# Graph convolution on one core: where the selection matrices are built, and for how many tiles edge_attr is loaded

## The chip, the cores and the metric

The kernel runs on one core of a Trainium2 chip. The metric is the device time of one execution in microseconds (us), the median of the runs shown. One further execution was taken with the hardware profiler; where the text speaks of a row, a wait or a timeline, it means that execution.

Five engines of the core take part. TensorE (PE in the profile, PEld for its weight loads) multiplies matrices into PSUM. VectorE (DVE) and ScalarE (ACT) do elementwise work. GpSimd (POOL) issues the gathers. SyncE (SP) issues most of the other transfers.

## The reference

One layer of a graph network. There are N = 12500 nodes with 160 features each (64 scalars and 32 vectors of 3), and 400000 edges, sorted by their target node.

```python
h_s, h_v = s @ lin1_ws / 8, v @ lin1_wv / sqrt(32)        # per node, times the node's attribute
w  = silu(edge_scalars @ fc_w1 / 8) @ fc_w2 / 8           # per edge: 64 -> 64 -> 224 weights
es, ev = h_s[edge_src], h_v[edge_src]
e0, e1 = edge_attr[:, :1], edge_attr[:, 1:4]
m_s1 = w1 * es * e0
m_s2 = w4 * (ev . e1) / 3
m_v1 = (w2 * es) (x) e1
m_v2 = w3 * ev * e0
m_v3 = w5 * cross(ev, e1) / 2
agg  = segment_sum(messages, edge_dst) / 4
pre  = self_connection(x) + lin2(agg)                     # per node
out  = layernorm(x + gated(pre))
```

(Scales and shapes are shortened. Layernorm has no learned weights.)

## The kernel before

**Tiles.** 128 edges are a tile, one edge in each partition. Five tiles (TB) are a block of 640 edges; there are 625 blocks. Since edges are sorted by target, the targets of a block fall into a window of W = 32 nodes, whose first node is computed on the chip. Four tiles are a quad (Q), and the main loop (L607) has one step for each quad, 782 in all. The quads are taken from chunks of 20 tiles: two sides of SIDE = 10 tiles each. A quad has two tiles of one side and two of the other, so that the two halves of the 128 partitions of `es` hold two runs of edges; a quad therefore usually touches two blocks. A chunk has 5 steps.

**Before the loop.** A table `h_tab` of all nodes' h is computed and written to DRAM. `rel`, for each edge the distance of its target from its block's first node, is computed once. The loop starts at about 113 us.

**A step n of the loop.** `hide(n + 1)` computes the hidden layer for a later step: the load of `es` (L278, on SP), two matmuls `ph` (L290), silu (L292). `gather` (L299) issues four indirect DMAs on GpSimd, one for each tile, into `hg`, a pool of four buffers. `weights` (L311) makes the 224 weights of each edge in PSUM: the tile `pw` has 128 x 4 x 256 numbers, of which columns 0 to 223 of each tile are used; there are two such buffers, of two banks each. `products` on VectorE multiplies `pw` and `hg` (L319, and three times L328) into `pr`. The multiplication by edge_attr and the sum over edges are one matmul: `sel` holds, for each edge and each of the four edge_attr components, a row of 32 numbers that is zero but for the column of its target, where it has the component. `add_tile` (L357) multiplies `sel` of a tile (as weights) with `pr` into the sums `pa` of a pair of blocks. This is done for the quad of the step before (`sum_up(*before)`), so that TensorE does pw(n) ahead of pa(n-1).

**Selection.** `select` works on one block: `oh` (L338) compares `rel` with 0 to 31 for five tiles, 128 x 160 numbers, into SBUF; `sel` (L341) multiplies that by edge_attr, 128 x 640 numbers. Four buffers of `sel` are kept. A list `order` says at which step a block is first needed. In each step, after the products and after the add below, blocks needed at once are selected; else one block is, if it is needed up to two steps ahead. So most steps have a selection and some have none.

**Closing a pair of blocks.** When a pair's sums are complete they are copied to SBUF (`sa`, L361), transposed (`pt` L369, copied as `tt` L370) in a later step, and every eight blocks the second linear map is applied (`po`, L378, copied as `os` L382). Then `add` (L387) adds one block a step to its window of `acc`, which holds the sums of all nodes in SBUF; the window's start is loaded into registers between L319 and L328.

**Finishing nodes.** When all blocks that reach a set of 512 nodes are added, `finish` handles it in pieces, one a step, by `go_on`: `turn` transposes 128 nodes of `acc` on TensorE (`pp`, L406) and scales them (`z`, L407), and then gates, residual, moments and normalization on VectorE and ScalarE follow, with a load of x (L394) and a store of the result (L437) on SP. There are 98 such turns. Every 30 steps a piece of the self connection is added to `acc` (L505 to L511).

**Loads of edge_attr.** For each group of 125 tiles `group` loads the indices of the gathers (L466) and, next to them, edge_attr (L468): 25 loads of 250 KB, with 2000 bytes in each partition.

**Order.** On TensorE, VectorE, ScalarE and GpSimd the instructions run in the order in which the program is written (`manual_schedule`, L603). SP runs its transfers in program order too, ahead of the others as far as the buffers allow. A redo path after the loop handles blocks whose targets don't fit into a window; it isn't entered with this data.

Of the kernel before, what the change touches and what calls it, by code (L numbers as in the profile page):

```python
# [10 lines left out]
F32 = mybir.dt.float32  # L11
I32 = mybir.dt.int32
# [3 lines left out]
OP = mybir.AluOpType  # L16
# [4 lines left out]
P = 128  # L21
# [4 lines left out]
TB = 5  # L26
BG = 25
EB = TB * P
EG = BG * EB
W = 32  # L30
Q = 4
SIDE = 2 * TB
# [4 lines left out]
NWT = 224  # L37
# [27 lines left out]
def gnn_kernel(  # L65
# [21 lines left out]
    nc = tc.nc  # L87
# [5 lines left out]
    GT = BG * TB  # L93
# [15 lines left out]
    for i in range(2):  # L109
        r = slice(S + i * V, S + (i + 1) * V)  # L110
# [204 lines left out]
    def products(pool, pw, hg, n, between=()):  # L315

        pr = pool.tile([P, Q, NPR], F32, name="pr")

        nc.vector.tensor_mul(  # L319
            pr[:, :n, 6 * V:10 * V].rearrange("p t (k c) -> p t k c", k=2),  # L320
            pw[:, :n, :2 * S].rearrange("p t (k c) -> p t k c", k=2),
            hg[:, :n, None, :S].to_broadcast([P, n, 2, S]))
        for f in between:
            f()

        for k, (first, step) in enumerate(((1, 2), (4, -2), (10, 1))):
            full = pr[:, :n, first * V:]
            nc.vector.tensor_mul(  # L328
                bass.AP(tensor=full.tensor, offset=full.offset,
                        ap=[full.ap[0], full.ap[1], [step * V, 3], [1, V]]),  # L330
                pw[:, :n, None, 2 * S + k * V:2 * S + (k + 1) * V].to_broadcast([P, n, 3, V]),
                hg[:, :n, S:].rearrange("p t (i c) -> p t i c", i=3))
        return pr

    def select(pool, r, e):

        oh = pool.tile([P, TB, W], F32, name="oh")
        nc.vector.tensor_tensor(oh, r[:, :, None].to_broadcast([P, TB, W]),  # L338
                                iota[:, None, :].to_broadcast([P, TB, W]), op=OP.is_equal)
        sel = pool.tile([P, TB, 4, W], F32, name="sel", bufs=4)  # L340
        nc.vector.tensor_mul(sel, oh[:, :, None, :].to_broadcast([P, TB, 4, W]),  # L341
                             e[:, :, :, None].to_broadcast([P, TB, 4, W]))
        return sel

    def cleared(psum):
# [5 lines left out]
    def add_tile(pa, sel, t, pr, start, stop):  # L351

        for k, (first, step, count) in enumerate(SUMS):
            span = pr[:, first * V:]
            a = bass.AP(tensor=span.tensor, offset=span.offset,
                        ap=[span.ap[0], [step[0] * V, count[0]], [step[1] * V, count[1]], [1, V]])
            nc.tensor.matmul(pa[k * W:(k + 1) * W], sel[:, t, k], a, start=start, stop=stop)  # L357
# [96 lines left out]
    with tc.tile_pool(  # L454
# [5 lines left out]
    ) as pa_ps, tc.tile_pool(name="misc_ps", bufs=2, space=PSUM) as misc_ps:  # L460
        groups = {}

        def group(g):
            if g not in groups:
                idx = loads.tile([P, GT], I32, name="idx")
                nc.sync.dma_start(idx, src[g])  # L466
                eat = loads.tile([P, GT, 4], F32, name="eat")
                nc.sync.dma_start(eat.rearrange("p t k -> p (t k)"),  # L468
                                  ea[g].rearrange("p t k -> p (t k)"))
                groups[g] = idx, eat  # L470
            return groups[g]

        def index(t):
            return group(t // GT)[0][:, t % GT:t % GT + 1]


        chunks = [((c, SIDE), (c + SIDE, SIDE)) for c in range(0, NB * TB - 2 * SIDE + 1, 2 * SIDE)]
# [8 lines left out]
        ess, hids = {}, {}  # L486
# [12 lines left out]

        CHN = 500  # L500

        def self_connection(c0):
# [10 lines left out]
        sels, order = {}, []  # L513
        for n, (_, _, tiles) in enumerate(steps):
            for t, _, _ in tiles:
                b = t // TB
                if b not in [x for _, x in order[-4:]]:
                    order.append((n, b))

        def choose(b):  # L520
            g, k = divmod(b, BG)
            sels[b] = select(edge, rel[:, b * TB:(b + 1) * TB],
                             group(g)[1][:, k * TB:(k + 1) * TB])

        left_of = {b: TB for b in range(NB)}
        pas = {}
# [33 lines left out]
        def sum_up(tiles, pr):  # L560
            for slot, (t, _, _) in enumerate(tiles):
                b = t // TB
                pa, place, blocks = sums_of(b)
                n = TB - left_of[b]
                last = n == TB - 1 and all(x == b or not left_of[x] for x in blocks)
                add_tile(pa[:, place], sels[b], t % TB, pr[:, slot], start=False, stop=last)
                left_of[b] -= 1
                if left_of[b] == 0:
                    sels.pop(b)
# [32 lines left out]

        with tc.manual_schedule(engines={ENG.PE, ENG.DVE, ENG.Activation, ENG.Pool}):  # L603
            hide(0)
            before = None
            pieces = list(range(0, N, CHN))
            for n, (c, i, tiles) in enumerate(steps):  # L607
                hide(n + 1)
                hg = gather(deep, [index(t) for t, _, _ in tiles])
                now, later = later, []  # L610
                pw = weights(pw_ps, hids[c, i // 2], [(half, u - i // 2 * 4) for _, half, u in tiles])
                ready = []
                pr = products(edge, pw, hg, len(tiles), [lambda: ready.extend(add_up(1))])
                for a in ready:
                    add(*a)

                need = [b for m, b in order if m <= n]
                todo = [b for _, b in order if b not in sels]
                for b in need:
                    choose(b)  # L620
                order = [(m, b) for m, b in order if b not in need]
                if not need and order and order[0][0] <= n + 2:
                    choose(order.pop(0)[1])
                go_on()
                for f in now:
                    f()
                if before is not None:
                    sum_up(*before)
                before = (tiles, pr)
                if n % 30 == 6 and pieces:  # L630
                    self_connection(pieces.pop(0))
            assert not pieces
            sum_up(*before)
            while later:
                later.pop(0)()
            while adds:
                for a in add_up(1):
                    add(*a)
            while doing or to_do:
                go_on()  # L640
# [88 lines left out]
```

## Time and profile before

| What | Value |
|---|---|
| Median of 3 runs (lowest to highest) | 5651.8 us (5649.6 to 5672.22) |
| Profiled execution, its own time | 5669.53 us |
| Its span | 5667.7 us |
| Mean granted clock of TensorE | 0.816 |
| TensorE busy (weight loads) | 74% (39%) |
| GpSimd busy | 54% |
| VectorE busy | 47% |
| ScalarE busy | 14% |
| Mean DMA traffic | 73 GB/s |

A row of the groups reads: line, engine, operation, what it writes and reads, partitions x elements, count; then the busy time in us and the mean length of one in ns; then how long the engine was idle just before these instructions, and what ended most of it. In a row of waits the numbers are the total in us, the number of waits and the longest. A line of the timeline has the start and the length in us, and in brackets the idle time ahead of it and what ended it. Idle time that "remote" ended is put down to no instruction of the records.

### The profile page before, as it was taken

Reading aid. Unit: us, or ns where it says so; the run is one execution under the profiler, and the core shown is the slowest. Engines: PE = TensorE matmul, PEld = TensorE weight load, DVE = VectorE, ACT = ScalarE, POOL = GpSimd, SP = SyncE. Lnnn points to the kernel's source line nnn. Section 1 sums busy time; section 2 is a strip of 40 time slices with the busy share of each in tenths; the row PEclk is TensorE's granted clock in tenths of the full one; section 3 lists DMA queues with packets and bytes.
Section 4 is the critical chain, followed back from the end, with each engine's and each line's share of the span. In section 5 each row is a group of like instructions: output and inputs, shape, how many; then the busy total and the mean of one; then the engine's idle time right before and its main releaser. Section 6 shows DMA issues by size and latency. Waiting matters only on the chain.

```text
span 5667.7 us, 89792 instructions
## 1 busy us (share of the span) xinstructions
PE 4182.8 (74%) x36179; PEld 2227.6 (39%) x36179; DVE 2642.3 (47%) x5628; ACT 809.3 (14%) x1639; POOL 3051.9 (54%) x3134
## 2 busy tenths in 40 slices
PE   6777777767777767777777777777776767777776
PEld 5334433333344434334333333433333433434343
DVE  4444444444444444444444444444444444444444
ACT  0111111111111111111111111111111111111111
POOL 3555555555555555555555555555555555555553
PEclk7788887888888878888888788887887888888787
DMA  6222222222222222222222222222222322232221
GB/s 172 68 72 73 72 72 66 73 74 65 76 76 67 74 68 74 74 70 74 72 74 73 63 76 69 73 77 68 75 72 63 82 67 73 71 79 69 68 69 46
DMA packets 232392, 416.39 MB, mean 73 GB/s; under 512 B 64580, under 2 KB 160592, under 8 KB 231713
## 3 DMA queue, kind: packets, MB, share of 16 engines
q0 software_dynamic: 150000, 256.20, 17.3%
q1 hardware_dynamic: 65972, 142.43, 9.9%
q10 hardware_dynamic: 15994, 11.93, 0.8%
q8 instruction: 285, 4.67, 0.3%
q14 instruction: 141, 1.16, 0.1%
HBM read 394.32 MB, written 16.00 MB: 72 GB/s over the span
## 4 chain that ended last, share of the span: by engine, by line
PE 31%; another core or an unknown queue 8%; issue 6%; DVE 3%; ACT 3%; DVEq 0%; DMA 0%; POOL 0%; ACTq 0%; POOLq 0%
PE pa L357 13%; PE pw L311 6%; PE ph L290 4%; PE po L378 3%; PE pt L369 2%; DVE pr L328 2%; ACT tt L370 1%; PE pa L348 1%; ACT hid L292 1%; DVE pr L319 0%; PE pp L406 0%; PE psc L510 0%; ACT L292 0%; DVEq L582 0%
## 5 line engine op out<-in xcount | busy, mean ns | idle before, releaser
L299 POOL DMA_INDIRECT hg<-h_tab,idx x3125 | 3029.5, 969 | 2562.8 <-DVE pr L328 962.0
L357 PE MATMUL pa<-pr,sel 128*32 128x192 f32 x25000 | 1813.8, 395 | 312.7 <-issue 298.8
L319 DVE TENSOR_TENSOR pr<-pw,hg 128x512 f32<-128x512 f32 x782 | 539.1, 689 | 2648.7 <-remote 1400.2
L357 PEld LDWEIGHTS pa<-pr,sel 128*32 128x32 f32 x25000 | 888.3, 127 | 1060.3 <-issue 768.8
L328 DVE TENSOR_TENSOR pr<-pw,hg 128x384 f32<-128x384 f32 x2346 | 1158.2, 549 | 5.7 <-issue 4.9
L311 PE MATMUL pw<-w,hid 64*128 64x224 f32 x6250 | 990.0, 429 | 48.3 <-issue 38.8
L369 PE MATMUL pt<-ident,sa 128*96 128x128 f32 x1250 | 317.8, 344 | 814.6 <-ACT tt L370 418.6
L311 PEld LDWEIGHTS pw<-w,hid 64*128 64x128 f32 x6250 | 645.2, 219 | 585.8 <-issue 530.2
L341 DVE TENSOR_TENSOR sel<-oh,eat 128x640 f32<-128x640 f32 x625 | 517.8, 828 | 168.2 <-PE pw L311 51.2
L290 PE MATMUL ph<-es,w 128*128 128x512 f32 x940 | 552.0, 673 | 10.8 <-issue 8.3
L369 PEld LDWEIGHTS pt<-ident,sa 128*96 128x96 f32 x1250 | 124.7, 144 | 1000.5 <-ACT tt L370 496.0
L361 ACT COPY sa<-pa 128x384 f32<-128x384 f32 x313 | 149.5, 478 | 2085.0 <-PE pa L357 1042.7
L292 ACT ACTIVATE hid<-ph 128x512 f32<-128x512 f32 (+1 forms) x470 | 247.0, 526 | 1242.9 <-PE ph L290 855.1
L378 PE MATMUL po<-tt,l 96*96 96x256 f32 (+1 forms) x1738 | 401.7, 383 | 9.6 <-issue 8.7
L378 PEld LDWEIGHTS po<-tt,l 96*96 96x96 f32 x1738 | 274.5, 164 | 127.1 <-issue 47.6
L370 ACT COPY tt<-pt 96x256 f32<-96x256 f32 x626 | 229.3, 366 | 588.0 <-PE pt L369 361.1
L290 PEld LDWEIGHTS ph<-es,w 128*128 128x128 f32 x940 | 165.8, 219 | 198.1 <-issue 184.7
L406 PE MATMUL pp<-ident,acc 96*128 96x96 f32 x196 | 44.9, 325 | 239.6 <-DVE acc L387 218.9
L338 DVE TENSOR_TENSOR oh<-rel,iota 128x160 f32<-128x160 int16 x625 | 196.3, 314 | 0.0
L382 ACT COPY os<-po 96x512 f32<-96x512 f32 (+1 forms) x79 | 45.6, 577 | 714.9 <-PE po L378 485.1
L387 DVE TENSOR_TENSOR acc<-acc,os 96x64 f32 x625 | 132.7, 212 | 12.6 <-ACT os L382 7.9
L406 PEld LDWEIGHTS pp<-ident,acc 96*128 96x128 f32 x196 | 23.8, 170 | 273.3 <-issue 187.5
(61 smaller groups left out, 794.7 us busy)
## 6 DMA issues: line engine op xcount, KB each, us to landing
es<-in_es_t_dram SPq DMA_DIRECT2D x312, 320.0 KB
hg<-h_tab,idx POOLq DMA_INDIRECT x3125
h_tab<-ht ACTq DMA_DIRECT2D x8, 960.0 KB
xt<-in_x_dram SPq DMA_DIRECT2D x24, 320.0 KB
out_dram<-y SPq DMA_DIRECT2D x24, 320.0 KB
eat<-in_ea_dram SPq DMA_DIRECT2D x25, 250.0 KB
xv<-in_xv_t_dram SPq DMA_DIRECT2D x25, 187.5 KB
xs<-in_xs_t_dram SPq DMA_DIRECT2D x25, 125.0 KB
```

What stands on the lines that cost most here:

```text
L290: nc.tensor.matmul(ph[:k, c], w1[:k, :k], es[:k, t0 * P + c0 * P:t0 * P + c1 * P], start=True, stop=True)
L292: nc.scalar.activation(hid[:k, c], ph[:k, c], AF.Silu, scale=1.0 / math.sqrt(64))
L299: nc.gpsimd.indirect_dma_start(out=hg[:, t, :], out_offset=None, in_=h_tab, in_offset=bass.IndirectOffsetOnAxis(ap=i, axis=0))
L311: nc.tensor.matmul(pw[:, t, :NWT], hid[r, c * P:(c + 1) * P], w2[r], start=True, stop=True)
L319: nc.vector.tensor_mul(pr[:, :n, 6 * V:10 * V].rearrange("p t (k c) -> p t k c", k=2), pw[:, :n, :2 * S].rearrange("p t (k c) -> p t k c", ...
L328: nc.vector.tensor_mul(bass.AP(tensor=full.tensor, offset=full.offset, ap=[full.ap[0], full.ap[1], [step * V, 3], [1, V]]), pw[:, :n, None ...
L338: nc.vector.tensor_tensor(oh, r[:, :, None].to_broadcast([P, TB, W]), iota[:, None, :].to_broadcast([P, TB, W]), op=OP.is_equal)
L341: nc.vector.tensor_mul(sel, oh[:, :, None, :].to_broadcast([P, TB, 4, W]), e[:, :, :, None].to_broadcast([P, TB, 4, W]))
L357: nc.tensor.matmul(pa[k * W:(k + 1) * W], sel[:, t, k], a, start=start, stop=stop)
L369: nc.tensor.transpose(pt[:, half, b], sa[:, b, half * V3:(half + 1) * V3], ident)
L370: nc.scalar.copy(tt[:, half, :, at_b:at_b + nb].rearrange("c k b n -> c b k n"), pt[:, half, :nb].rearrange("c b (k n) -> c b k n", k=4))
L378: nc.tensor.matmul(po[:, k, :nb], l2[:, terms[to, part, half]], tt[:, half, part, :nb], start=(n == 0), stop=(n == len(of) - 1))
```

## The change

The kernel after has a new function `select_quad`, which does the selection of just the quad of the step. The one-hot numbers of its four tiles (128 x 128) are written into columns 224 to 255 of the same `pw` tile in PSUM that holds the quad's weights. From there `sel` is made in two instructions, one for each side (two tiles, 128 x 256 numbers each), with edge_attr as the other input; `sel` has two buffers now. It stands straight after the products and ahead of the add. The list of blocks to be selected and the selection ahead are gone; a step's `sel` goes with its `pr` to `sum_up`. `select` remains for the redo path, with one buffer each.

Edge_attr is loaded for a chunk of 20 tiles at a time by `load_parts`, into three buffers, right behind the chunk's two loads of `es` on SP: 326 loads, of which 300 have ten tiles of one side (128 rows of 160 bytes). Indices are still loaded for 125 tiles.

```diff
     def select(pool, r, e):
-        oh = pool.tile([P, TB, W], F32, name="oh")
+        oh = pool.tile([P, TB, W], F32, name="oh", bufs=1)
...
-        sel = pool.tile([P, TB, 4, W], F32, name="sel", bufs=4)
+        sel = pool.tile([P, TB, 4, W], F32, name="sel1", bufs=1)
...
+    def select_quad(pool, pw, tiles, eat):
+        n = len(tiles)
+        step = tiles[-1][0] - tiles[0][0] - 1 if n == Q else 1
+        r = rel[:, tiles[0][0]:]
+        sides = 2 if n == Q else 1
+        each = n // sides
...
+        nc.vector.tensor_tensor(
+            pw[:, :n, NWT:].rearrange("p (h u) w -> p h u w", h=sides),
+            bass.AP(tensor=r.tensor, offset=r.offset, ap=[r.ap[0], [step, sides], [1, each], [0, W]]),
+            iota[:, None, None, :].to_broadcast([P, sides, each, W]), op=OP.is_equal)
+        sel = pool.tile([P, Q, 4, W], F32, name="sel")
+        for h in range(sides):
+            k = slice(h * each, (h + 1) * each)
+            u = tiles[h * each][2]
+            nc.vector.tensor_mul(
+                sel[:, k], pw[:, k, None, NWT:].to_broadcast([P, each, 4, W]),
+                eat[:, h, u:u + each, :, None].to_broadcast([P, each, 4, W]))
+        return sel
...
-        def group(g):
-            if g not in groups:
-                idx = loads.tile([P, GT], I32, name="idx")
-                nc.sync.dma_start(idx, src[g])
-                eat = loads.tile([P, GT, 4], F32, name="eat")
-                nc.sync.dma_start(eat.rearrange("p t k -> p (t k)"),
-                                  ea[g].rearrange("p t k -> p (t k)"))
...
+        def load_parts(sides):
+            eat = loads.tile([P, 2, SIDE, 4], F32, name="eat", bufs=3)
+            for half, (t, n) in enumerate(sides):
+                at_t = 0
+                while at_t < n:
+                    g, k = divmod(t + at_t, GT)
+                    m = min(n - at_t, GT - k)
+                    nc.sync.dma_start(eat[:, half, at_t:at_t + m], ea[g, :, k:k + m])
+                    at_t += m
+            return eat
...
                 ess[c] = load_hidden(loads, edges)
+                eats[c] = load_parts(chunks[c])
...
-                add_tile(pa[:, place], sels[b], t % TB, pr[:, slot], start=False, stop=last)
+                add_tile(pa[:, place], sel, slot, pr[:, slot], start=False, stop=last)
...
                 pr = products(edge, pw, hg, len(tiles), [lambda: ready.extend(add_up(1))])
+                sel = select_quad(edge, pw, tiles, eats[c])
                 for a in ready:
                     add(*a)
-
-                need = [b for m, b in order if m <= n]
-                todo = [b for _, b in order if b not in sels]
-                for b in need:
-                    choose(b)
-                order = [(m, b) for m, b in order if b not in need]
-                if not need and order and order[0][0] <= n + 2:
-                    choose(order.pop(0)[1])
                 go_on()
...
-                    sum_up(*before)
-                before = (tiles, pr)
+                    sum_up(*before)
+                before = (tiles, pr, sel)
```

More of the change, by code (lines that the diff above doesn't have):

```diff
@@ L335, in select @@
     def select(pool, r, e):
-        oh = pool.tile([P, TB, W], F32, name="oh")
+        oh = pool.tile([P, TB, W], F32, name="oh", bufs=1)
         nc.vector.tensor_tensor(oh, r[:, :, None].to_broadcast([P, TB, W]),
                                 iota[:, None, :].to_broadcast([P, TB, W]), op=OP.is_equal)
-        sel = pool.tile([P, TB, 4, W], F32, name="sel", bufs=4)
+        sel = pool.tile([P, TB, 4, W], F32, name="sel1", bufs=1)
         nc.vector.tensor_mul(sel, oh[:, :, None, :].to_broadcast([P, TB, 4, W]),
                              e[:, :, :, None].to_broadcast([P, TB, 4, W]))
+        return sel
[5 more added lines that the diff above has]
+        each = n // sides
+        assert [t - tiles[0][0] for t, _, _ in tiles] == [h * step + u for h in range(sides) for u in range(each)]
+        nc.vector.tensor_tensor(
[9 more added lines that the diff above has]
+                eat[:, h, u:u + each, :, None].to_broadcast([P, each, 4, W]))
         return sel
@@ L461, in gnn_kernel, with index @@
         groups = {}
-        def group(g):
+        def index(t):
+            g = t // GT
             if g not in groups:
-                idx = loads.tile([P, GT], I32, name="idx")
-                nc.sync.dma_start(idx, src[g])
-                eat = loads.tile([P, GT, 4], F32, name="eat")
-                nc.sync.dma_start(eat.rearrange("p t k -> p (t k)"),
-                                  ea[g].rearrange("p t k -> p (t k)"))
[L470 to L474, printed above, removed]
+                groups[g] = loads.tile([P, GT], I32, name="idx")
+                nc.sync.dma_start(groups[g], src[g])
+            return groups[g][:, t % GT:t % GT + 1]
+        def load_parts(sides):
[8 more added lines that the diff above has]
+            return eat
         chunks = [((c, SIDE), (c + SIDE, SIDE)) for c in range(0, NB * TB - 2 * SIDE + 1, 2 * SIDE)]
@@ L484, in gnn_kernel @@
                 steps.append((c, i, [(sides[half][0] + u, half, u) for half, u in slots]))
-        ess, hids = {}, {}
+        ess, eats, hids = {}, {}, {}
         def hide(n):
@@ L511, in self_connection @@
                 nc.vector.tensor_add(acc[:, k, c0:c0 + cn], acc[:, k, c0:c0 + cn], p[:, :cn])
[L513 to L523, printed above, removed]
         left_of = {b: TB for b in range(NB)}
@@ L558, in output, with sum_up @@
             adds.extend((b, os, k) for k, b in enumerate(blocks))
-        def sum_up(tiles, pr):
+        def sum_up(tiles, pr, sel):
             for slot, (t, _, _) in enumerate(tiles):
@@ L565, in sum_up @@
                 last = n == TB - 1 and all(x == b or not left_of[x] for x in blocks)
-                add_tile(pa[:, place], sels[b], t % TB, pr[:, slot], start=False, stop=last)
+                add_tile(pa[:, place], sel, slot, pr[:, slot], start=False, stop=last)
                 left_of[b] -= 1
                 if left_of[b] == 0:
-                    sels.pop(b)
                     for k, (p, blocks) in enumerate(pair):
```

## The prediction

> **What bounds the kernel now.** First the page's busy times, to see whether any engine is full.
>
> ```profile
> PE 4182.8 (74%) x36179; PEld 2227.6 (39%) x36179; DVE 2642.3 (47%) x5628; ACT 809.3 (14%) x1639; POOL 3051.9 (54%) x3134
> PE 31%; another core or an unknown queue 8%; issue 6%; DVE 3%; ACT 3%; DVEq 0%; DMA 0%; POOL 0%; ACTq 0%; POOLq 0%
> ```
>
> None is. The second line is the chain that ended last: TensorE leads it, VectorE has 3%. So work added on VectorE counts only where TensorE or GpSimd waits for it. Next, the page's costliest groups: the gathers, and the five VectorE groups that a step runs.
>
> ```profile
> L299 POOL DMA_INDIRECT hg<-h_tab,idx x3125 | 3029.5, 969 | 2562.8 <-DVE pr L328 962.0
> L319 DVE TENSOR_TENSOR pr<-pw,hg 128x512 f32<-128x512 f32 x782 | 539.1, 689 | 2648.7 <-remote 1400.2
> L341 DVE TENSOR_TENSOR sel<-oh,eat 128x640 f32<-128x640 f32 x625 | 517.8, 828 | 168.2 <-PE pw L311 51.2
> L406 PE MATMUL pp<-ident,acc 96*128 96x96 f32 x196 | 44.9, 325 | 239.6 <-DVE acc L387 218.9
> L338 DVE TENSOR_TENSOR oh<-rel,iota 128x160 f32<-128x160 int16 x625 | 196.3, 314 | 0.0
> L387 DVE TENSOR_TENSOR acc<-acc,os 96x64 f32 x625 | 132.7, 212 | 12.6 <-ACT os L382 7.9
> ```
>
> The loop runs 782 steps from about 113 us on, so a step takes about 7.05 us. VectorE stands idle 2648.7 us before the first product of a step (3.4 us each): the cover for what the change adds to it. GpSimd needs 4 gathers, each 0.95 us and a gap of 0.30, 5.0 us a step: it is not the bound either. "Remote" before L319 is not this step's gather, which landed 13 us or more earlier; it is TensorE's signal for pw, recorded as issued and not yet answered. Third, the waits:
>
> ```profile
> DVE pr L319 <- remote: 1400.2, 267, 19.1
> PE pp L406 <- DVE acc L387: 218.9, 66, 8.5
> ```
>
> Columns are total us, times, longest. The second line is the only large wait of TensorE on an operation that the change moves: 66 waits of 3.3 us. Last, the timeline of one step with such a wait (start, length, engine and line):
>
> ```profile
> 3001.59 0.69 DVE L319 TENSOR_TENSOR pr<-pw,hg 128x512 f32<-128x512 f32 x1 [6.50 <-PE pw L311]
> 3002.28 1.49 DVE L328 TENSOR_TENSOR pr<-pw,hg 128x384 f32<-128x384 f32 x3
> 3003.69 0.21 DVE L387 TENSOR_TENSOR acc<-acc,os 96x64 f32 x1
> ...
> 3004.05 0.56 PE L406 MATMUL pp<-ident,acc 96*128 96x96 f32 x2 [3.60 <-DVE acc L387]
> ...
> 3004.53 2.79 PE L357 MATMUL pa<-pr,sel 128*32 128x192 f32 x32
> ...
> 3008.19 1.03 PE L311 MATMUL pw<-w,hid 64*128 64x224 f32 x8
> 3009.86 0.69 DVE L319 TENSOR_TENSOR pr<-pw,hg 128x512 f32<-128x512 f32 x1 [4.80 <-PE pw L311]
> ```
>
> The add releases the transpose pp at once; TensorE, held 3.60 us, then does pa, ph, pw in order, and the next products wait for that pw. Here add, pp, pa, pw, pr is a closed ring: a later add is a later next step.
>
> Two kinds of steps matter for the rivals. In about 484 of 750 that I sorted, GpSimd is idle when the products end; the next products come about 5.5 to 5.9 us later. In 266 GpSimd is still in a burst of gathers; the signal of pw then comes late and the step takes about 9.2 us. Whether selection has a part in it is the main uncertainty. An overlap shows in the timeline:
>
> ```profile
> 3047.63 0.82 DVE L341 TENSOR_TENSOR sel<-oh,eat 128x640 f32<-128x640 f32 x1
> ...
> 3047.86 1.41 POOL L299 DMA_INDIRECT hg<-h_tab,idx  x1 [0.30 <-issue]
> ...
> 3051.02 0.69 DVE L319 TENSOR_TENSOR pr<-pw,hg 128x512 f32<-128x512 f32 x1 [1.38 <-remote]
> ```
>
> The gather beside the selection took 1.41 us where the usual one takes 0.946, and pw, issued at 3047.75, is answered only at 3051.0.
>
> **What the Trainium skill says.** "SBUF — State Buffer", Who interferes with whom: a VectorE instruction with two SBUF inputs contends with a GpSimd instruction that reads SBUF, one with at most one does not, and TensorE waits on neither. The trace agrees for sel (both inputs in SBUF, gather 1.41 us); oh and the add, also with two, stretch no gather. "VectorE: DVE Perf Modes", The perf-mode tier table: fp32 tensor_tensor runs at 1x from SBUF or PSUM alike. The rows agree: 512 elements from PSUM 689 ns, 640 from SBUF 828 ns lie on one line. "PSUM — Partial Sum Buffer", PSUM bank collisions: engines may not meet in one bank. pw(n+1) lies in other banks than pw(n), so no new wait of this kind arises. "DMA: Bandwidth & Descriptors", Specifications: full rate needs 512 bytes or more; the new rows of edge_attr have 160. No run shows yet what that costs here.
>
> **The change, part by part.**
>
> VectorE's work. The rows 64, 160, 384, 512, 640 elements at 212, 314, 549, 689, 828 ns give about 143 ns and 1.07 ns an element. The new one-hot (128 elements) is 0.28 us, each half of sel (256) 0.417 us: 1.12 us in each of 782 steps, 873 us, against 196.3 + 517.8 = 714 before. The 160 us more lie under the 2648.7 us of idle time: taken as 0 in themselves; without that cover they cost 160.
>
> The add moves behind one-hot and sel: 0.28 + 0.83 and two short gaps of about 0.06 us between dependent operations, 1.25 us later after the products. What is queued behind it on VectorE is the finishing work of go_on, off the path; who waits for it is pp. 66 recorded waits, up to 82 with those recorded at pp's weight load; take 72 x 1.25 = +90 us. Ends: 0, if pa absorbs it, and 98 turns x 1.25 = +123. I take +90, because in these steps nothing lies beside the ring.
>
> pa(n) now needs sel of its own quad, which ends about 3.5 us after the products begin (2.2 for the products, 1.25). Before, sel was ready up to two steps ahead. TensorE does ph, pw and pa of the step before in between, so usually it comes later anyway: in the trace, the first pa of a step starts under 3.5 us after its products began in 96 of 750 steps, with 68 us lacking in all. Range 0 to +68; I take +20, since much of it overlaps the pp case. Queued behind a waiting pa are ph and pw of the next steps. Two waits of pa a step, one for each half, replace about one; they cost the issue of an instruction each, nothing that I can see.
>
> pw is now released by sel instead of the products, 1.2 us later. Two buffers exist, and pa(n) stands before pw(n+2) on TensorE and itself waits for sel(n): no new wait.
>
> Buffers of sel: VectorE's 168.2 us of idle time before L341 (waiting for pa) go, off the path: 0.
>
> GpSimd. sel's second input comes from SBUF, its first from PSUM, so it should no longer stretch gathers. All gathers together last 3029.5 - 3125 x 0.946 = 73 us more than the median, about 65 of it beside sel. One-hot still has two SBUF inputs, but ends 0.3 us after the products, just as the freed gather begins. Range 0 to -73 from this alone; I take -40, as GpSimd has 1739 us of idle time before its quads.
>
> edge_attr: 25 loads of 250 KB become 326, of which 300 have 128 x 40 elements; the bytes stay. SP issues them after the same chunk's es loads, about 30 us ahead of use, and its queue is otherwise idle; 326 x 0.5 us of issue is 163 us of SP spread over the span. The index loads behind them have longer lead still. They share the engines with the gathers, which have 13 us of slack. 0 while the lead holds; if each chunk's rows held the gathers 0.5 us past their slack, 157 x 0.5 = +80. A gain from it I exclude: nothing waits for eat now.
>
> Sum: 0 + 90 + 20 - 40 + 0 = +70 us. The profiled execution took 5669.5 us (span 5667.7 and 1.8 around it), so 5740 there; the median of the runs shown, 5651.8, lies 18 below it, so 5720.
>
> **The rivals.**
>
> B, faster: the collision of sel with the gathers is what makes pw's signal late. For it: of the 150 steps without a selection 3 to 5% are late, of those with one 45 to 49%; and in the first 10 us of the loop eight gathers in a row run beside prompt signals until the first sel. Against it: selections and gathers both follow the products, so they meet whatever the cause; a few late steps have no selection near the gathers (3463 to 3470 us: po stands unanswered 6.8 us, VectorE idle); the skill has TensorE wait on neither; and the one-hot still has two SBUF inputs. Late steps cost about 9.2 - 5.9 = 3.3 us, 250 of them 820 us. All cured: 5652 + 110 - 820, about 4940; half: about 5350; a fifth: 5600. It decides from 110 us (the losses above) and 28 us (0.5%) on, 0.55 us a late step.
>
> C, no change: pp's delay is absorbed, as pa of the step before could anyway run no earlier for lack of GpSimd's next gathers, and the relief cancels the rest: about 5650. Against: GpSimd is idle in the timeline of the turn.
>
> D, worse: pa waits for sel in all prompt steps. 484 x 0.5 us is 242 more than I count: 5960. Against: the 68 us counted above.
>
> **How the numbers follow.** My case, slower: 0.52, its own range 5680 to 5840 (at most all losses and no relief, 5652 + 123 + 68; at least about half the losses, 60, and 30 of relief). B 0.30, of which about a third beyond half cured. C 0.14. D 0.04. The range 5420 to 5830 leaves out B's far part, D and a little of my own tail. 0.5%, 28 us, is about what a measurement of this kernel can tell from no change: faster 0.31, same 0.15, slower 0.54.
>
> **What would show it.** Right: the wait of pp on the add is near 4.5 us a time instead of 3.3; the halves of sel near 0.417 us and one-hot 0.28; gathers of over 1 us mostly gone; and the "remote" idle time before L319 still above 1200 us. Wrong by B: that idle time falls by hundreds of us, the count of steps over 8 us with it. Wrong by D: pa shows idle time for sel in most steps, where its row now has 6.6 us for the products. Wrong by edge_attr: "remote" or sel waits for eat, or gathers that land within 2 us of their use.

## The result and the profile after

The kernel after takes 5880.9 us (median of 4 runs, 5857 to 5901); the kernel before, with one more run beside it, 5654.2 us. The ratio is 1.039 (interval 1.035 to 1.044): slower by 227 us, the direction that was forecast, but above the range of 5420 to 5830. The profiled execution of the kernel after took 5857.3 us, its span 5855.6, 188 us more than before.

One thing has to be known for all that follows. The experiments ran in five groups, each with runs of the kernel before beside it, and the groups are of two kinds. On the first kind, to which the prediction's profile and the result belong, the unchanged kernel before takes 5650 to 5780 us, and in its two profiles VectorE waits 1400 and 1499 us in all for signals of TensorE put down to "remote". On the second kind the same program takes 4216 us; it was not profiled there, but the profiles of the other kernels there have no "remote" wait at all. The expectations below speak of kinds of chips. That the kind belongs to the chip is not shown: the chips are numbered in the runs, and the numbers 0 and 11 each appear in one group of either kind. Each experiment is set against the runs of the kernel before in its own group.

The page of the kernel after, busy times and the chain that ended last:

```profile
PE 4139.0 (71%) x36179; PEld 2218.3 (38%) x36179; DVE 2803.9 (48%) x6723; ACT 806.3 (14%) x1639; POOL 2997.5 (51%) x3134
PE 46%; another core or an unknown queue 20%; issue 13%; DVE 9%; POOL 5%; ACT 5%; DMA 1%; DVEq 1%; ACTq 0%; POOLq 0%; SPq 0%
```

VectorE is busy 162 us longer, GpSimd 54 us less; TensorE leads the chain as before. The costliest groups of the same page:

```profile
L299 POOL DMA_INDIRECT hg<-h_tab,idx x3125 | 2975.1, 952 | 2804.0 <-DVE pr L328 1874.1
L319 DVE TENSOR_TENSOR pr<-pw,hg 128x512 f32<-128x512 f32 x782 | 538.9, 689 | 2732.0 <-remote 1547.0
L362 DVE TENSOR_TENSOR sel<-pw,eat 128x256 f32<-128x256 f32 x1563 | 590.6, 419 | 27.1
L428 PE MATMUL pp<-ident,acc 96*128 96x96 f32 x196 | 49.4, 352 | 295.3 <-DVE acc L409 279.6
L354 DVE TENSOR_TENSOR pw<-rel,iota 128x128 f32<-128x128 int16 x782 | 234.9, 300 | 26.8
L409 DVE TENSOR_TENSOR acc<-acc,os 96x64 f32 x625 | 132.8, 213 | 11.3 <-ACT os L404 6.2
```

The halves of sel take 419 ns, one-hot 300 ns. The mean gather fell from 969 to 952 ns, close to its median, so the gathers are no longer stretched; yet the idle time that "remote" ends did not fall, it rose from 1400 to 1547 us. GpSimd's own row gives the whole difference: its gathers take 54 us less (3029.5 before), and its idle time ahead of them is 241 us more (2562.8 before), which makes 187 of the 188 us. The waits:

```profile
DVE pr L319 <- remote: 1547.0, 265, 19.0
PE pp L428 <- DVE acc L409: 279.6, 70, 9.1
PEld pp L428 <- DVE acc L409: 103.1, 20, 9.5
PEld pa L379 <- DVE sel L362: 70.7, 102, 3.1
PE pa L379 <- DVE sel L362: 34.2, 35, 2.7
```

The transpose pp waits longer for the add (3.3 us a time before, 4.0 now), and pa has a new wait, for the sel of its own quad. (Rows of PE and PEld can count the same stretch of time twice.) A step with such a transpose, from the timeline:

```profile
3090.66 0.69 DVE L319 TENSOR_TENSOR pr<-pw,hg 128x512 f32<-128x512 f32 x1 [5.68 <-PE pw L311]
3091.37 1.49 DVE L328 TENSOR_TENSOR pr<-pw,hg 128x384 f32<-128x384 f32 x3
3092.89 0.30 DVE L354 TENSOR_TENSOR pw<-rel,iota 128x128 f32<-128x128 int16 x1
...
3093.22 0.76 DVE L362 TENSOR_TENSOR sel<-pw,eat 128x256 f32<-128x256 f32 x2
3093.89 0.21 DVE L409 TENSOR_TENSOR acc<-acc,os 96x64 f32 x1
...
3094.25 0.55 PE L428 MATMUL pp<-ident,acc 96*128 96x96 f32 x2 [3.64 <-DVE acc L409]
```

The add starts 3.23 us after the products begin; in the step shown of before it was 2.10. Sorted by kind, the steps with a transpose (85 and 86 of them as I sort) lengthened from 8.62 to 9.47 us, 73 us together; the others lengthened from 6.86 to 7.01 us, 104 us together.

### The profile page after: what moved, and what is told of

Its sections match the earlier page's. It is cut to its first block, busy times and chain, and to the rows that moved or that the text cites. A ratio compares the mean times of both kernels' runs of the same rounds, so it can differ in the third digit from the quotient of the medians.

```text
span 5855.6 us, 91179 instructions
## 1 busy us (share of the span) xinstructions
PE 4139.0 (71%) x36179; PEld 2218.3 (38%) x36179; DVE 2803.9 (48%) x6723; ACT 806.3 (14%) x1639; POOL 2997.5 (51%) x3134
## 3 DMA queue, kind: packets, MB, share of 16 engines
q14 instruction: 152, 1.25, 0.1%
## 4 chain that ended last, share of the span: by engine, by line
PE 46%; another core or an unknown queue 20%; issue 13%; DVE 9%; POOL 5%; ACT 5%; DMA 1%; DVEq 1%; ACTq 0%; POOLq 0%; SPq 0%
PE pa L379 19%; PE pw L311 9%; PE ph L290 6%; PE po L400 5%; POOL hg L299 5%; DVE pr L328 5%; PE pt L391 3%; DVE sel L362 1%; ACT tt L392 1%; ACT hid L292 1%; PE pa L370 1%; DVE pr L319 1%; DVE pw L354 1%; ACT sa L383 1%
## 5 line engine op out<-in xcount | busy, mean ns | idle before, releaser
L299 POOL DMA_INDIRECT hg<-h_tab,idx x3125 | 2975.1, 952 | 2804.0 <-DVE pr L328 1874.1
L379 PE MATMUL pa<-pr,sel 128*32 128x192 f32 x25000 | 1780.8, 395 | 322.3 <-issue 283.4
L319 DVE TENSOR_TENSOR pr<-pw,hg 128x512 f32<-128x512 f32 x782 | 538.9, 689 | 2732.0 <-remote 1547.0
L328 DVE TENSOR_TENSOR pr<-pw,hg 128x384 f32<-128x384 f32 x2346 | 1158.9, 549 | 6.9 <-issue 5.2
L391 PE MATMUL pt<-ident,sa 128*96 128x128 f32 x1250 | 328.1, 353 | 991.8 <-ACT tt L392 532.0
L311 PE MATMUL pw<-w,hid 64*128 64x224 f32 x6250 | 963.9, 424 | 34.2 <-issue 27.6
L311 PEld LDWEIGHTS pw<-w,hid 64*128 64x128 f32 x6250 | 632.5, 217 | 557.9 <-issue 499.8
L362 DVE TENSOR_TENSOR sel<-pw,eat 128x256 f32<-128x256 f32 x1563 | 590.6, 419 | 27.1
L391 PEld LDWEIGHTS pt<-ident,sa 128*96 128x96 f32 x1250 | 128.0, 147 | 1185.5 <-ACT tt L392 608.0
L354 DVE TENSOR_TENSOR pw<-rel,iota 128x128 f32<-128x128 int16 x782 | 234.9, 300 | 26.8
```

The costliest lines, as they stand in the source:

```text
L299: nc.gpsimd.indirect_dma_start(out=hg[:, t, :], out_offset=None, in_=h_tab, in_offset=bass.IndirectOffsetOnAxis(ap=i, axis=0))
L311: nc.tensor.matmul(pw[:, t, :NWT], hid[r, c * P:(c + 1) * P], w2[r], start=True, stop=True)
L319: nc.vector.tensor_mul(pr[:, :n, 6 * V:10 * V].rearrange("p t (k c) -> p t k c", k=2), pw[:, :n, :2 * S].rearrange("p t (k c) -> p t k c", ...
L328: nc.vector.tensor_mul(bass.AP(tensor=full.tensor, offset=full.offset, ap=[full.ap[0], full.ap[1], [step * V, 3], [1, V]]), pw[:, :n, None ...
L354: nc.vector.tensor_tensor(pw[:, :n, NWT:].rearrange("p (h u) w -> p h u w", h=sides), bass.AP(tensor=r.tensor, offset=r.offset, ap=[r.ap[0 ...
L362: nc.vector.tensor_mul(sel[:, k], pw[:, k, None, NWT:].to_broadcast([P, each, 4, W]), eat[:, h, u:u + each, :, None].to_broadcast([P, each ...
```

## Experiments

**Theories.** W: the loss is waiting, pp for the add and pa for sel. G: the gathers, no longer stretched, run unbroken, and TensorE's late signals end only when they land. E: the small loads of edge_attr. Later L: the loss needs the late signals of the first kind.

**Undo the order, undo PSUM, undo the loads.** Three kernels take back one part each of the kernel after. The first:

```diff
-                sel = select_quad(edge, pw, tiles, eats[c])
                 for a in ready:
                     add(*a)
+                sel = select_quad(edge, pw, tiles, eats[c])
```

> The kernel after, with the add of a block put back ahead of the selection. Theory W (waits: the add and pa come later): the 86 steps with a transpose pp grew from 8.62 to 9.47 us, about 75 us; they should come back, about 5805 us, with pp's wait on the add back near 219 us. Theory G (gathers that are no longer stretched run unbroken, and pw's signal comes only when they land) and theory E (the small loads of edge_attr): no change, 5880.

In the second the one-hot numbers go into a tile of SBUF:

```diff
-            pw[:, :n, NWT:].rearrange("p (h u) w -> p h u w", h=sides),
+            oq[:, :n].rearrange("p (h u) w -> p h u w", h=sides),
...
-                sel[:, k], pw[:, k, None, NWT:].to_broadcast([P, each, 4, W]),
+                sel[:, k], oq[:, k, None, :].to_broadcast([P, each, 4, W]),
```

> The kernel after, with the one-hot numbers in an SBUF tile instead of the pw banks, so that both inputs of sel come from SBUF again. Theory G: gathers beside sel are stretched again (several hundred over 1 us, against 45), late steps shorten from 9.8 towards 9.3 us, and the time falls by about 100 us to 5780. Theories W and E: no change, within 25 us of 5880. Old rival B (collisions make the signal late) would have it slower, by 60 us or more.

The third loads edge_attr by groups of 125 tiles as before, and reads it from there (a half that lies across two groups is made in two instructions):

```diff
-                eat[:, h, u:u + each, :, None].to_broadcast([P, each, 4, W]))
...
+                    eat(g)[1][:, o:o + m, :, None].to_broadcast([P, m, 4, W]))
...
-                eats[c] = load_parts(chunks[c])
...
-                sel = select_quad(edge, pw, tiles, eats[c])
+                sel = select_quad(edge, pw, tiles, group)
```

> The kernel after, with edge_attr loaded for 125 tiles at a time as before (25 loads), the selection being a quad at a time from PSUM still. Theory E: most of the 227 us come back, 5700 or less. Theories W and G: no change, within 25 us of 5880.

The fourth changes the kernel before: the add ahead of the products.

```diff
-                ready = []
-                pr = products(edge, pw, hg, len(tiles), [lambda: ready.extend(add_up(1))])
-                for a in ready:
+                for a in add_up(1):
                     add(*a)
+                pr = products(edge, pw, hg, len(tiles))
```

> The kernel before, with the add of a block put ahead of the step's products instead of behind them. If pp's waits for the add (66 of 3.3 us, 219 us) lie on the path, as theory W has it, most of it is gained: 5450 to 5550. If what follows in those steps is bound elsewhere anyway, about 5640.

This group was of the second kind, which none of the expectations had foreseen: before 4216.5 us. So none of their times in us can be held against it. Measured, as ratios to it: add first 0.980 (0.979 to 0.982); one-hot in SBUF 1.0065 (1.005 to 1.008); edge_attr in groups 1.0021 (1.0014 to 1.0028); before with the add early 0.988 (0.987 to 0.990), so that the add's place behind the products was worth 49 us in the kernel before already. What the first three say of the change needs the kernel after on the same kind, next.

**The kernel after on the second kind, and two versions of it.**

> The kernel after, unchanged, beside the kernel before on the chip of this call. The earlier experiments ran on a chip where the kernel before took 4216 us and no wait of VectorE was put down to 'remote', against 5654 and 1400 us. If the loss of 3.9% lies in waits of the program (theory W), it is there on such a chip too: 1.02 to 1.04 times before. If it lies in the late signals of the first chip (theory L), the ratio on a chip without them is that of the run with edge_attr in groups, 1.00 to 1.01; on a chip like the first it is 1.035 to 1.045.

The next has the add ahead of the products, as in the fourth above, in the kernel after.

> The kernel after, with the add ahead of the step's products (and so ahead of the selection). Theory W: pp never waits for selection or products; at least the 2% that the add ahead of the selection alone gained against the kernel after, so a ratio to before of 0.97 to 0.98 on a chip like that of the earlier experiments, 1.00 to 1.02 on one like the first. If pp's wait was not on the path: that of the kernel after.

The last has the one-hot in SBUF as in the second above, the add first, and selects in step n for step n + 1, with three buffers of `sel`; the main edit is:

```diff
-                sel = select_quad(edge, pw, tiles, eats[c])
                 for a in ready:
                     add(*a)
+                sel = nxt
+                if n + 1 < len(steps):
+                    nxt = select_quad(edge, pw, steps[n + 1][2], eats[steps[n + 1][0]])
```

> The kernel after, with the one-hot in SBUF, the add first, and the selection of a quad made one step ahead, so that no pa waits for the sel of its own quad. Theory W: the waits of pa for sel (some 500 us of weight loads and matmuls in the run with the add first) are replaced by shorter ones for the products; 1 to 2% below the run with the add first (0.9803 of before on that chip): 0.96 to 0.975. If GpSimd's gathers bound the steps anyway: 0.975 to 0.985. On a chip like the first: 0.99 to 1.02.

Measured: the kernel after 1.0024 (1.0017 to 1.0032), 4228.2 us; add ahead of the products 0.969 (0.967 to 0.970), 4085.9 us; selection a step ahead 0.990 (0.988 to 0.991), 4175.1 us. So on the second kind the change does almost nothing, where theory W had 2 to 4% of loss and L 0 to 1%. L's number came, but not for L's reason, since the parts of the change do something here too. The waits of pp, of the kernel after and of the one with the add first, on this kind:

```profile
PE pp L428 <- DVE acc L409: 312.3, 76, 8.9
```

```profile
PE pp L428 <- DVE acc L409: 241.5, 75, 9.1
```

The add's place behind the selection costs 4228.2 - 4133.8 = 94 us; the 92 steps with a transpose are 8.77 us long with it and 7.39 without, 127 us together, of which the other steps take some 30 back. It reaches the time through GpSimd's idle time, in the same two kernels:

```profile
L299 POOL DMA_INDIRECT hg<-h_tab,idx x3125 | 2974.5, 952 | 1184.1 <-issue 811.2 <-DVE pr L328 164.1 <-DMA eat<-in_ea_dram 95.8
```

```profile
L299 POOL DMA_INDIRECT hg<-h_tab,idx x3125 | 2974.9, 952 | 1084.5 <-issue 807.3 <-DMA eat<-in_ea_dram 94.3 <-DVE sel L362 72.8
```

The gathers take the same time in both; the 100 us of idle time are the loss (99 us between these two profiles). The gain that pays it back is in the gathers. Their rows, of the kernel before with the add early and then of the kernel after with the add early, the closest pair that differs in the selection and the loads but not in the add:

```profile
L299 POOL DMA_INDIRECT hg<-h_tab,idx x3125 | 3047.6, 975 | 1046.7 <-issue 956.8 <-DMA hg<-h_tab,idx 32.6 <-DVE pr L328 16.1
```

```profile
L299 POOL DMA_INDIRECT hg<-h_tab,idx x3125 | 2967.3, 950 | 1047.7 <-issue 812.2 <-DMA eat<-in_ea_dram 96.0 <-DVE sel L362 51.8
```

Here GpSimd issues one gather after another: the idle time ahead of the gathers is the same 1047 us in both, all of it the 0.3 us between two and the 95 us ahead of the first one. The gathers take 80 us less, and the time is 82 us less (4167.6 and 4085.9). In this pair a nanosecond of a gather is a nanosecond of the kernel. With the one-hot in SBUF the gathers took 30 us more than in the kernel after and the time was 17 us more, so sel's two SBUF inputs by themselves stretch gathers. They do not make up the 80 us: the rest lies in what else differs in that pair, above all the smaller pieces of sel and their place in the step, which were not separated. The version with the selection a step ahead missed both of its forecasts; it lost to the one with the add first (0.990 against 0.980), its gathers taking 43 us more and the time being 41 us more. That pa no longer waits for its own sel there gained nothing that shows: TensorE waits ahead of pa for VectorE 308 us with the add first and 312 us here, now for the products instead of sel. Edge_attr in groups and by chunks differ by 3 us (4225.1 and 4228.2): theory E falls on the second kind. In the direction of theory G nothing was seen, but there are no late signals on this kind. On the first kind neither G nor E was tried.

**More TensorE work in both.** To make TensorE the bound on either kind, the weights' matmuls are done three times over, with the same result:

```diff
-            nc.tensor.matmul(pw[:, t, :NWT], hid[r, c * P:(c + 1) * P], w2[r],
-                             start=True, stop=True)
+            for _ in range(3):
+                nc.tensor.matmul(pw[:, t, :NWT], hid[r, c * P:(c + 1) * P], w2[r],
+                                 start=True, stop=True)
```

> The kernel before, unchanged, for its trace on the chip of this call. Expected on a chip like that of the last two calls: 4217 us, no 'remote' time ahead of the products, gathers issued one after the other for nearly the whole span (GpSimd the bound: 3125 gathers of 0.946 us with gaps of 0.30 are 3894 us), and about 70 us of stretched gathers. On a chip like the first: 5650 and 1400 us of 'remote'.

> The kernel before, with the matmuls of the weights done three times over (the same result into the same place), some 2 us more TensorE work a step, so that TensorE and not GpSimd is the bound on any chip. Only a base for the next two: on a chip like that of the last calls 5000 to 5700 us.

> The kernel after, with the same extra TensorE work. Theory W (the loss is waits of TensorE for the add and for sel, and shows where TensorE is the bound): 1.02 to 1.04 times the kernel before with the extra work, though the two plain kernels differ by 0.2% on this kind of chip. Theory L (it needs the late signals of the first chip): 0.995 to 1.005 times.

> The kernel after with the add put back ahead of the selection, with the same extra TensorE work. Theory W: the part of the loss that pp's wait makes comes back, 1 to 2%; what remains against the kernel before with the extra work, 0.5 to 2%, is the wait of pa for the sel of its own quad. Theory L: the same as the kernel before with the extra work, or below it by up to 2%.

This group was of the first kind (before 5771 us; the kernel before once more 1.0012 of it, 0.999 to 1.0035). With the extra work, before took 6542 us, after 6842, after with the add first 6691; to the plain kernel before that is 1.132 (1.126 to 1.137), 1.183 (1.176 to 1.190) and 1.159 (1.155 to 1.164), and to the first of the three 1.046 and 1.023. The waits of pp in these three, in that order:

```profile
PE pp L407 <- DVE acc L388: 170.7, 66, 4.5
```

```profile
PE pp L429 <- DVE acc L410: 244.2, 66, 5.6
```

```profile
PE pp L429 <- DVE acc L410: 177.7, 68, 5.2
```

The wait grows by 1.1 us a time, as the working of the prediction had it, and goes back with the order. Theory L had no loss with the extra work on the second kind, which did not come about; that the loss is here, with the waits for late signals down from 1499 to 313 us in the kernel before, speaks against it. By kind of step, sorted here by the order of TensorE's work, the steps with a transpose make 130 us of the 308 that the span grew, and the add first gives them all back. Another 142 us sit in the 274 steps that have transposes of a pair's sums (L391) and no pp, at 8.99 us before and 9.51 after; most of it stays (9.42) with the add first. The expectation had what stays as pa's wait for its own sel. It is not that: in the two versions of the kernel after pa starts 3.6 us or more after its products, about when its sel is done, and the rows have at most 0.7 us of waits of pa for sel and 4.2 for one-hot.

The granted clock goes the same way, but it does not suffice. Its mean is 0.889, 0.865 and 0.880 in the three. The records have full and half speed only, so a stretch's time at half speed is 2 x (1 - clock) of it. In each of the 274 steps that is 2.16, 2.53 and 2.34 us. At most half of a time at half speed is lost, so the clock is worth at most 0.19 us of the 0.52 that such a step grew, and 0.09 of the 0.43 with the add first (estimates from these figures). What grew by about as much as the steps is something else: pauses of TensorE inside the weights that follow in such a step. Intervals of over 0.5 us from the start of one of these matmuls to the next number 406 in the kernel before (298 us in all), 520 after (430 us) and 513 with the add first (409 us), and the records name nothing that the matmul waited for. Why there are more of them is open. In the plain profiles they did not grow: 134 such intervals (86 us) before, 102 (56 us) after. So the extra work shows the part of the loss that pp's wait makes, and this other part is not the plain kernel's.

**The versions again, for the first kind.** Three kernels ran once more, in a group that was again of the second kind.

> The kernel after with the add ahead of the selection, once more, for a chip like the first (where before takes 5650 to 5780 us), on which it was not yet run. Theory W: of 3.9% the part of pp's wait comes back, 75 to 130 us: 1.015 to 1.027 times before there. Theory L (the loss has nothing to do with the add): 1.035 to 1.045. On a chip like that of the second call: 0.980 again.

> The kernel after with the add ahead of the products, once more, for a chip like the first. Theory W: pp waits for neither selection nor products, which is worth up to 66 x 3.3 = 219 us more than the wait was in the kernel before; on a chip like the first 0.98 to 1.01 times before. Theory L: 1.03 or more. On a chip like that of the second call: 0.969 again.

> The kernel after with the one-hot in SBUF, the add first and the selection a step ahead, once more, for a chip like the first. If what is left of the loss there, with the add first, is pa's wait for the sel of its own quad (about 60 us more of such waits than before), this is 1.00 to 1.01 times before; if it is the lack of stretched gathers or the clock, it stays at 1.015 to 1.027. On a chip like that of the second call: 0.990 again.

Measured 0.980, 0.969 and 0.990: the earlier ratios to within 0.001. The last group was of the first kind (before 5782 us):

> The kernel before with the weights' matmuls three times over, again, as the base of the next two on the chip of this call. On a chip where before takes 5650 to 5780 us: 1.13 times before again. On one where it takes 4217: TensorE gets some 1.0 to 2.0 us more a step than GpSimd's 5.0 us leave room for; 4900 to 5600 us.

> The kernel after with the same extra TensorE work. If it is TensorE being the bound that makes the loss, whatever the chip: 1.02 to 1.05 times the base of this call also where the plain kernels differ by 0.2%. If it needs the first kind of chip: 1.00 to 1.01 on the second kind, 1.046 on the first.

> The kernel after with the add ahead of the products, with the same extra TensorE work. If pp's wait for the add is on TensorE's path: pp no longer waits, 5% or more below the run before it, that is at or below the base: 0.97 to 1.00 times the base. If only the part behind the selection counts: 1.02 times the base, as the add ahead of the selection gave.

> The kernel after with the add ahead of the products, plain. On a chip where before takes 4217 us: 0.969 of it a third time. On a chip like the first: 0.98 to 1.01 if the wait of pp is what the loss comes from, 1.03 or more if not.

With the extra work: before 6568, after 6831 (1.040 of it), after with the add ahead of the products 6518 (0.9925). So the expectation for the early add came true. What the kernel after would do with extra work on the second kind was not seen, since both groups with it were of the first. With the add early the wait that the prediction had named is gone:

```profile
L429 PE MATMUL pp<-ident,acc 96*128 96x96 f32 x196 | 41.4, 301 | 4.9 <-DVE acc L410 4.5 <-DVE z L430 0.4
```

The plain kernel with the add ahead of the products takes 5770.7 us, 0.9977 of before (0.9968 to 0.9986). With the extra work, where both stand in one group, moving the one instruction takes back the whole loss. Plain, it stands against the 1.039 of the result, which comes from other runs: the kernel after was not run plain in this group, nor was this one profiled. Nor is it the size of what the change did to pp alone, because the kernel before has 219 us of these waits as well, which the early add removes too, as far as the run with extra work shows; the two were not measured apart, plain, on the first kind. The kernel after with the add early beats the kernel before on both kinds, by 3.1% on the second and by 0.2% on the first.

## Why the prediction was wrong, step by step

**VectorE's work: right.** 0.28 and 0.417 us forecast, 0.300 and 0.419 measured; 160 us more, measured 162; covered, as L319 still has 2732 us of idle time ahead of it. It agrees with "VectorE: DVE Perf Modes", The perf-mode tier table, which has fp32 tensor_tensor at 1x from PSUM as from SBUF: sel with one input in PSUM (419 ns) lies on the line of the other rows (417). Of the five groups that the prediction calls VectorE's, L406 is TensorE's, and L328, VectorE's largest with 1158 us, is not among them; none of its sums uses that.

**The add behind the selection: right in mechanism and place, its size near.** +90 forecast; 73 us in the profiles of the first kind, 94 us by the order undone on the second, 130 us in the steps concerned with the extra work. The add was late by 1.13 us in the steps shown instead of 1.25.

**pa's wait for its own sel: too small as a wait.** +20 was taken out of 0 to 68. The stretches in which pa or its weight load waits for VectorE are 95 us in all after and 42 before: 53 more. (The rows alone, 70.7 and 34.2 for sel, count part of it twice.) What they cost in time isn't settled: without the wait for sel, on the second kind, nothing was gained, and in the runs with extra work there is next to none.

**The relief of the gathers: the step that failed.** The gathers did what was forecast (time over their median from 77 to 20 us). But -40 was credited to a kernel in whose profile GpSimd has some 1750 us of idle time ahead of its quads, and that idle time was even given as the reason for about half of it. It says rather that the relief is worth nothing there; the credit belonged at 0. The profiles of the first kind are in line with that: the gathers took 54 us less, GpSimd's idle time grew by 241 us, and the time did not fall. The relief was not undone alone on that kind, so its 0 there is argued. Where GpSimd is the bound, on the second kind, it is worth all of its 80 us. With 0 here the sum is 73 us for pp and between 0 and 53 for pa, 73 to 126 instead of 70, still short of 188 in the profiles: the credit accounts for 40 of the 118 us that were missing.

**The rest, 60 to 115 us of the profiles: open.** It sits in the steps without pp, 6.86 us long before and 7.01 after, a term that the prediction's sum did not have. But in the later group of the first kind these steps take 7.03 us in the kernel before too, and its profile is 5786.6 us long; against it the steps with a transpose are all that the kernel after adds (8.62 to 9.47). So this part may be a difference between groups and not between kernels; the kernel after was not run plain beside before in those groups. If it is, what the change costs on the first kind is nearer to 1.2% of the time, the 69 us between those two profiles, than to 3.9%.

**edge_attr: right.** Nothing, shown by the loads undone on the second kind (3 us). On the first kind they were not undone; the waits there name such a load once, ahead of the first gather, where in the kernel before another load stands.

**The rivals.** B fell in the profile: the stretched gathers are gone and "remote" has not shrunk (1547 against 1400 us); steps whose products start over 2 us after the end of pw are 303 against 297. C came true on the second kind, for another reason: loss and relief cancel there, each at 80 to 94 us. D's wait came, at 53 of the 242 us that it was priced at. What no rival had was that the program has a second regime. The range should also have reached further up: its top was about the sum of the largest losses, 123 + 68, on steps of which a third were not understood.

## What to carry to other kernels

Before work is put into an engine's queue, look for an instruction behind it that another engine waits for, and let that one go first: here a short add, moved ahead of work that it doesn't need, was worth 142 us on the second kind, more than the 80 us that the change relieves there. A relief on an engine counts only where that engine has no idle time: 80 us of gathers were worth 82 us where GpSimd was the bound, and some were wrongly credited where it was not.

## What the runs showed that was not expected

The same program took 4216 us in some groups of runs and 5650 to 5780 in others, with a mean granted clock of 0.92 and 0.81. The kernel after, profiled on both kinds, moves the same packets and its gathers take the same time. What differs is the "remote" waits, of which the profiles of the second kind have none: "remote" ends 1499.4 us of the idle time before L319 in the kernel before on the first kind.

```profile
DVE pr L319 <- remote: 1499.4, 272, 19.2
```

With the weights' matmuls three times over, in the same group, it ends only a fifth of that:

```profile
DVE pr L320 <- remote: 312.6, 61, 17.1
```

The granted clock rose from 0.811 to 0.889 with more work. What makes the signals late is open. The stretched gathers are not the cause: with them gone there were 1547 us of such waits, and on the second kind stretched gathers are there without one such wait.

"SBUF — State Buffer", Who interferes with whom, says that a VectorE instruction with two SBUF inputs contends with a GpSimd instruction that reads SBUF, and one with at most one does not. The runs agree for sel: with one input in PSUM it leaves the gathers alone (mean 952 ns, 950 with the add early), and with two in SBUF it stretches them (961 and 966 ns in the two versions that had it). One-hot, which still has two SBUF inputs, stretches none to speak of in these profiles.
